# Two-layer graph attention: the last division of layer 1 in two parts, stepped along with the output projection, and the last output rows stored 128 at a time

## The chip, the cores and the metric

The kernel runs on one core of a Trainium2 chip. The metric is the device time of one execution in microseconds, as the median of several runs. All data are 32-bit floats.

## The reference

x is 4096 x 512, adj is 4096 x 4096. Both layers are residual attention layers over 4096 nodes with eight heads of 64. Cut to what matters here, which is the second layer (the first has the same outline, with additive scores):

```python
h = relu(layernorm(x))
keys, queries, values = h @ Wks, h @ Wqs, h @ Wvs        # per head: 4096 x 64
atts = queries @ keys.T / 8 - 1e16 * (1 - max(adj, I))   # per head: 4096 x 4096
atts = softmax(atts)
x = x + einsum('hqm,hmk,hko->qo', atts, values, Wo)      # sum over heads, 512 -> 512
```

## The kernel before

**Names.** TensorE (PE) does matmuls, VectorE (DVE), ScalarE (ACT) and GpSimd (POOL) the elementwise work, and every DMA of this part is issued by SyncE (SP), whose queue is worked in order: a DMA that waits for a semaphore holds all that stand behind it.

**Layer 1's main loop.** The eight heads are worked as `HC` = 4 pairs c. For each pair the 4096 queries are cut into `NG` = 32 groups of 128, and each group into `GS` = 4 sets of 32 queries, so there are `SETS` = 128 sets per pair and `total` = 512 sets. The order of the whole layer is written out by hand: one loop over steps s, in which a set goes through scores on PE (`scores`, L997), mask and minimum on DVE (`masked`, L1013), the exponential on ACT (`exps`, L1050, which also leaves the row sums in the tile `sums`), transposes on DVE and PE (`squares`, L1057; `turned`, L1065), and the product with the values (`weighted`, L1083) on PE. The product runs `PROD` = 8 steps behind, so n = s - 8 is the set that it works. After a group's four sets `finish` (L1092, L1093) copies the undivided result, transposed, to `att_d[c]` in DRAM. The penalties of a set (`a`, 512 KB, L963) are fetched 5 steps ahead.

**The division.** The softmax denominators are applied afterwards, for half a pair (16 groups, 2048 queries) at a time, by a generator `divided(c, half)` that does one small piece at each call of `next`. `inverted` sums the row sums across partitions with a matmul by `bands` into `tot` (L1098) and takes the reciprocal on DVE (L1103); at the next call it transposes the result on PE (L1106), copies it on ACT (L1108) and writes it to `inv_d` in DRAM with two DMAs (L1110). `scaled` then handles four blocks of 512 queries in two pairs of blocks: it loads the block of `att_d` (L1122, 256 KB) and the inverses, broadcast to 64 partitions, with two DMAs (L1124), each block at a call of its own; then multiplies both blocks (L1131); then stores both back to `att_d` (L1134). The multiplications are done by POOL, but by DVE in the very last division. A half costs eleven calls. A division starts at each n with n % 64 == 1 (n > 1), that is one step after its half is complete, and every step of the loop makes one call. Seven of the eight halves so lie inside the loop; the eighth, pair 3's second half, starts at s = 521, and the loop ends with s = 522, after two of its eleven calls.

**The projection.** `projected(j)` makes 128 output rows (tile j of `NB` = 32): eight PE instructions (four matmuls of 128 x 512, each recorded as two) into a PSUM tile `oo` (L1166; the pool has four buffers), then the residual is added on DVE (L1169). Two tiles make a chunk. A chunk's inputs, `at` (L1154, 512 KB of `att_d`, all pairs) and `xt` (L1156, 512 KB), are fetched by `load_chunk`, which is called three times at s = 508 to 510 and afterwards after each odd tile, which also stores the chunk's 256 rows (L1171, 512 KB). So chunk i + 3 is fetched when chunk i is done. Tiles 0 to 9 are made inside the loop (s = 513 to 522), tiles 10 to 31 in a plain loop after it. Chunks 0 to 7 cover groups 0 to 15, whose division is done early. Before `load_chunk` fetches chunk 8 or a later one, it first runs every division that is still open to its end, which for the eighth half means its nine open calls, all in a row:

```python
if i >= NG // 2 // ZR:
    for d in divisions:
        for _ in d:
            pass
    divisions.clear()
```

Chunk 8 is fetched after tile 11, in the plain loop. The functions that the diff touches, and their callers:

Of the kernel before, what the change touches and what calls it, by code (L numbers as in the profile page):

```python
# [15 lines left out]
P = 128  # L16
# [7 lines left out]
def kernel(  # L24
# [14 lines left out]
    nc = tc.nc  # L39
    N, DM = x.shape  # L40
    H, D = src_proj.shape[1:]
    HD = H * D
    NB = N // P
    KC = DM // P
    HC = HD // P
# [16 lines left out]
    SQ = 32  # L62
# [3 lines left out]
    bands = const.tile([P, P], F32, name="bands")  # L66
# [34 lines left out]
    with tc.tile_pool(name="a0k", bufs=1) as pk, tc.tile_pool(name="a0v", bufs=4) as pv, tc.tile_pool(  # L101
# [361 lines left out]
        def step(n):  # L463
            return groups[n // 2], n % 2

        with tc.manual_schedule():
            NQ = NB // XR
            rows = [load_rows(0)]
# [10 lines left out]
            made = []  # L479
# [10 lines left out]
            for q in range(NQ + 3):  # L490
                n = q - 3
# [8 lines left out]
                if n in (2, 4, 6):  # L500
                    for h in range(2):
                        cols = bass.ts(n // 2 - 1, 2 * XR * P)
# [29 lines left out]
            for s in range(total + 6):  # L532
                G, h = step(s) if s < total else (None, 0)
                for half in range(2):
# [3 lines left out]
                    n = 2 * s + half - LEAD  # L538
                    turn = 0 <= n < 2 * total
                    if turn:  # L540
                        T, i = groups[n // HALVES], n % HALVES
# [11 lines left out]
                    if half == 1 and s + 1 < total:  # L553
                        leaky(*step(s + 1))

                        c, at = divmod(s + 3, 2 * NB)
# [11 lines left out]
                    if 1 <= n <= 2 * total:  # L568
                        W, w = groups[(n - 1) // HALVES], (n - 1) % HALVES
# [13 lines left out]
    GS = P // SQ  # L583
    NG = NB
# [6 lines left out]
    with tc.tile_pool(name="b0c", bufs=1) as pc, tc.tile_pool(name="b0a", bufs=4) as pa, tc.tile_pool(  # L591
# [250 lines left out]
        with tc.manual_schedule():  # L842
# [4 lines left out]
            for s in range(SETS + PROD + 10):  # L847
                if s + AHEAD < SETS:
                    adjs[s + AHEAD] = load_adj(*step(s + AHEAD))
                n = s - PROD  # L850
# [20 lines left out]
                if s % 2 and s < SETS:  # L871
                    G, k = step(s)
# [3 lines left out]
                if s % 2 == 0 and 0 <= s - 2 < SETS:  # L876
                    G, k = step(s - 2)
# [3 lines left out]
                if 0 <= n < SETS:  # L881
                    W, w = step(n)
# [7 lines left out]
    inv_d = dram.tile([HC, 2, N], F32, name="inv_d")  # L890
# [15 lines left out]
    SG = NG // 2  # L906
    with tc.tile_pool(name="a1t", bufs=1) as pt, tc.tile_pool(name="a1k", bufs=4) as pkk, tc.tile_pool(
# [9 lines left out]
        sums = pt.tile([P, HC, 2, 2, SG, GS], F32, name="sums")  # L917
# [174 lines left out]
            nc.scalar.copy(oT, G.o[:, :P])  # L1092
            nc.sync.dma_start(att_d[G.c, :, bass.ts(G.g, P)], oT)  # L1093

        def inverted(c, half):

            tot = pm.tile([P, 512], F32, tag="ms", name="tot")
            nc.tensor.matmul(  # L1098
                tot[:, : 2 * SG * GS], lhsT=bands,
                rhs=sums[:, c, half].rearrange("p h g k -> p (h g k)"), start=True, stop=True,  # L1100
            )
            inv = px.tile([P, P], F32, tag="oT", name="inv")
            nc.vector.reciprocal(inv[:SQ], tot[:SQ, : 2 * SG * GS])  # L1103
            yield
            invT = pm.tile([P, 512], F32, tag="ms", name="invT")
            nc.tensor.transpose(invT[:, :SQ], inv[:SQ], ident[:SQ, :SQ])  # L1106
            rows = px.tile([P, SQ], F32, name="rows")
            nc.scalar.copy(rows, invT[:, :SQ])  # L1108
            for h in range(2):
                nc.sync.dma_start(  # L1110
                    inv_d[c, h, bass.ts(half, SG * P)].rearrange("(q i) -> q i", i=SQ), rows[bass.ts(h, D)]
                )
            yield

        def scaled(c, half):

            last = (c, half) == (HC - 1, 1)
            zs = []
            for i in range(4):
                cols = bass.ts(half * 4 + i, 4 * P)  # L1120
                z = pz.tile([P, 2, 4 * P], F32, tag="z", name="z")
                nc.sync.dma_start(z[:, 0], att_d[c, :, cols])  # L1122
                for h in range(2):
                    nc.sync.dma_start(z[bass.ts(h, D), 1], inv_d[c, h, cols].partition_broadcast(D))  # L1124
                yield
                zs.append((cols, z))
                if i % 2 == 0:
                    continue
                yield
                for cols, z in zs:  # L1130
                    (nc.vector if last else nc.gpsimd).tensor_mul(z[:, 0], z[:, 0], z[:, 1])  # L1131
                yield
                for cols, z in zs:
                    nc.sync.dma_start(att_d[c, :, cols], z[:, 0])  # L1134
                zs = []

        def divided(c, half):
            yield from inverted(c, half)
            yield from scaled(c, half)

        ZR = 2
        chunks = []

        def load_chunk():

            i = len(chunks)
            if i >= NG // 2 // ZR:
                for d in divisions:
                    for _ in d:
                        pass  # L1150
                divisions.clear()
            if i < NB // ZR:
                at = pat.tile([P, HC, ZR * P], F32, name="at")
                nc.sync.dma_start(at, att_d[:, :, bass.ts(i, ZR * P)].rearrange("c p n -> p c n"))  # L1154
                xt = pa.tile([P, ZR, DM], F32, tag="a", name="xt")
                nc.sync.dma_start(xt, x1_d[bass.ts(i, ZR * P), :].rearrange("(r p) d -> p r d", p=P))  # L1156
                chunks.append((at, xt))

        def projected(j):
            if j >= NB:  # L1160
                return
            i, r = divmod(j, ZR)
            at, xt = chunks[i]
            o = psc.tile([P, HF], F32, tag="sc", name="oo")
            for c in range(HC):
                nc.tensor.matmul(  # L1166
                    o, lhsT=at[:, c, bass.ts(r, P)], rhs=wot[:, c, :], start=(c == 0), stop=(c == HC - 1)
                )
            nc.vector.tensor_add(xt[:, r], xt[:, r], o)  # L1169
            if r == ZR - 1:  # L1170
                nc.sync.dma_start(out[bass.ts(i, ZR * P), :].rearrange("(r p) d -> p r d", p=P), xt)  # L1171
                load_chunk()

# [14 lines left out]
        with tc.manual_schedule():  # L1188
            pens = {}

            def prefetch(n):
                if n < total:
                    if n % (QG * GS) == 0:
                        load_queries(n // (QG * GS))
                    pens[n] = penalty(*step(n))

            AHEAD = 5
            rb = 0
            divisions = []
            load_keys(0)  # L1200
            for n in range(AHEAD):
                prefetch(n)
            for n in range(2):
                without_self(*step(n), pens[n])
                made_penalty(*step(n), pens[n])
            for i in range(GS):
                load_values(0, i)
            for s in range(total + PROD + 3):
                if s + 2 < total:
                    without_self(*step(s + 2), pens[s + 2])  # L1210
                if s < total:
                    keep_penalty(*step(s), pens[s])

                c, at = divmod(s + 4, SETS)
                if 0 < c < HC and at == 0:
                    load_keys(c)
                c, at = divmod(s - PROD - 1 + GS, SETS)
                if 0 < c < HC and at < GS:
                    load_values(c, at)
                turn = 0 <= s - TURN < total  # L1220
                if turn:
                    squares(*step(s - TURN))
                turn = turn and (s - TURN) % 2

                if s % 2 and 0 <= s - 3 < total:
                    G, k = step(s - 3)
                    smallest(G, k // 2)
                if turn:
                    tr = turned(*step(s - TURN))
                n = s - PROD  # L1230
                if 0 < n <= total and n % GS == 0:
                    finish(groups[n // GS - 1])
                if s > total:
                    projected(rb)
                    rb += 1
                if s < total:
                    scs = scores(*step(s))
                    masked(*step(s), scs, pens.pop(s))
                if turn:
                    taken(*step(s - TURN), tr)  # L1240
                if 0 <= s - EXPS < total:
                    exps(*step(s - EXPS))
                if s + 2 < total:
                    made_penalty(*step(s + 2), pens[s + 2])
                if s % 2 and s < total:
                    G, k = step(s)
                    parted(G, k // 2)
                if 0 <= n < total:
                    W, w = step(n)
                    weighted(W, w)  # L1250
                if n > 1 and n % (SG * GS) == 1:
                    divisions.append(divided(*divmod(n // (SG * GS) - 1, 2)))
                for d in divisions[:1]:
                    if next(d, d) is d:
                        divisions.pop(0)
                if s == (HC - 1) * SETS + SETS // 2:
                    wot = pkk.tile([P, HC, DM], F32, tag="k", name="wot")
                    nc.sync.dma_start(wot, wo.rearrange("h d o -> (h d) o").rearrange("(c p) o -> p c o", p=P))
                if s > total - AHEAD and len(chunks) < 3:
                    load_chunk()  # L1260
                prefetch(s + AHEAD)

            for j in range(rb, NB):
                projected(j)


# [26 lines left out]
```

## Time and profile before

| what | us |
|---|---|
| median of three runs | 4854.54 |
| fastest and slowest of them | 4853.94, 4856.94 |
| the profiled execution, its own time | 4850.36 |
| its span, from the first to the last instruction | 4848.6 |
| PE busy | 4663.8 (96%) |
| DVE busy | 4440.2 (92%) |
| ACT busy | 3833.9 (79%) |
| POOL busy | 440.3 (9%) |

The profiled execution lasted 1.8 us longer than its span, and 4.2 us less than the median of the runs. All start times below are microseconds from the span's start. Layer 1's loop fills the stretch from 2472 on; the tiles after the loop begin at 4757.8. In rows of the timeline the first two numbers are the start and the duration of a group of like instructions; what stands in brackets is the time for which the engine had been idle before it, and what ended that. In the table by stretches, the columns are the stretch, its length, then busy time and number of instructions for PE, PE's weight loads, DVE, ACT and POOL, and at last the granted clock of PE (1.00 is full), the share of the DMA engines, and the GB/s that they moved.

### The profile page before, as it was taken

The page shows a single profiled execution, that of the slowest core. Times are in us where ns is not written, and L with a number is a line of the kernel's source. Part 1 is how long each engine was busy: PE and PEld are TensorE (multiplying, and loading weights), DVE is VectorE, ACT ScalarE, POOL GpSimd, SP SyncE. Part 2 cuts the span into 40 slices and gives each one's busy share as a digit, 9 for nine tenths or more (in the row PEclk, how much of TensorE's full clock was granted, in tenths as well). Part 3 has the DMA queues.
Part 4 walks back from the last instruction along what each step waited for, and adds up shares of the span by engine and source line. Part 5 has one row for each costly group of instructions (what it writes and reads, how often), then busy time and mean ns, then how long its engine had stood idle before and what let it go on. Part 6 is the DMA issues. An engine that isn't in the chain of part 4 may idle for free.

```text
span 4848.6 us, 145764 instructions
## 1 busy us (share of the span) xinstructions
PE 4663.8 (96%) x62099; PEld 3480.4 (72%) x62099; DVE 4440.2 (92%) x7787; ACT 3833.9 (79%) x4300; POOL 440.3 (9%) x999
## 2 busy tenths in 40 slices
PE   8999999999999959999989999999999999999998
PEld 7888888888888847777756666666666666666664
DVE  7999999999999898988759999999999999999981
ACT  6999999999999898888648888666666666666660
POOL 2000000000000011100123343000000000000000
PEclk9999999999999979999999999999999999999999
DMA  7444544445444384444377787534344343544435
GB/s 267 151 165 152 183 169 161 158 150 202 162 157 150 119 183 141 148 140 146 107 224 253 251 277 262 183 130 152 136 161 158 132 158 129 192 132 139 154 123 196
DMA packets 358556, 818.49 MB, mean 169 GB/s; under 512 B 60048, under 2 KB 179088, under 8 KB 332816
## 3 DMA queue, kind: packets, MB, share of 16 engines
q1 hardware_dynamic: 357904, 809.16, 50.7%
q8 instruction: 486, 7.96, 0.7%
q14 instruction: 166, 1.36, 0.1%
HBM read 668.21 MB, written 140.77 MB: 167 GB/s over the span
## 4 chain that ended last, share of the span: by engine, by line
PE 61%; DVE 14%; ACT 13%; issue 8%; DMA 3%; SPq 1%; POOL 0%; DVEq 0%; ACTq 0%; POOLq 0%
PE o L1083 20%; PE sc L997 19%; ACT t L173 6%; PE tr L1065 5%; PE mp L793 5%; DVE t L163 5%; DVE pT L197 4%; ACT t L152 4%; ACT pT L195 2%; PE bo L716 2%; PE tr L186 2%; PE o L208 2%; DVE bt L669 2%; PE oo L1166 2%; DVE bt L708 2%
## 5 line engine op out<-in xcount | busy, mean ns | idle before, releaser
L1013 DVE CUSTOM_DVE_ANT_0 t<-sc,a 128x512 f32<-128x512 f32 x2048 | 1284.3, 682 | 88.9 <-PE sc L997 67.0
L1083 PEld LDWEIGHTS o<-t,v 128*64 128x64 f32 x16384 | 883.8, 137 | 428.4 <-issue 344.7
L1050 ACT ACTIVATE t<-t,nm 128x1024 f32<-128x1024 f32 x1024 | 1166.0, 1143 | 4.2 <-DVE nm L1039 3.6
L997 PE MATMUL sc<-k,q 64*32 64x512 f32 x16384 | 1004.5, 596 | 5.5 <-DVE nm L1013 5.4
L1083 PE MATMUL o<-t,v 128*64 128x128 f32 x16384 | 1007.4, 276 | 0.5 <-ACT oT L1092 0.4
L1057 DVE STREAM_TRANSPOSE t<-t 128x1536 f32<-128x1536 f32 x512 | 907.4, 1772 | 7.9 <-ACT t L1050 7.6
L163 DVE CUSTOM_DVE_ANT_0 t<-t,a 128x2048 f32<-128x2048 f32 x384 | 876.7, 2283 | 22.6 <-ACT t L152 18.3
L186 PE MATMUL tr<-ident,t 128*128 128x128 f32 x6144 | 779.2, 277 | 30.1 <-ACT pT L195 20.2
L208 PE MATMUL o<-pT,v 128*64 128x128 f32 x12288 | 757.1, 276 | 1.1 <-DVE pT L197 1.0
L186 PEld LDWEIGHTS tr<-ident,t 128*128 128x128 f32 x6144 | 662.6, 141 | 121.4 <-issue 65.5
L173 ACT ACTIVATE t<-t,nm 128x4096 f32<-128x4096 f32 x192 | 730.7, 3806 | 11.8 <-DVE nm L168 11.6
L152 ACT ACTIVATE t<-tb,src 128x4096 f32<-128x4096 f32 (+1 forms) x193 | 731.0, 3788 | 2.2 <-DVE tb L408 2.2
L1072 ACT COPY t<-tr 128x1024 f32<-128x1024 f32 x256 | 259.1, 1012 | 591.2 <-PE tr L1065 591.1
L208 PEld LDWEIGHTS o<-pT,v 128*64 128x64 f32 x12288 | 664.4, 137 | 62.0 <-issue 47.9
L197 DVE COPY pT<-tr 128x1024 f32<-128x1024 f32 x549 | 653.2, 1215 | 9.8 <-PE tr L186 9.8
L997 PEld LDWEIGHTS sc<-k,q 64*32 64x32 f32 x16384 | 251.6, 106 | 383.0 <-issue 331.0
L669 DVE CUSTOM_DVE_ANT_0 bt<-lk,ba 128x1024 f32<-128x1024 f32 x256 | 302.7, 1219 | 64.1 <-ACT e L799 45.3
L659 ACT ACTIVATE lk<-tb,srcb 128x1024 f32<-128x1024 f32 x256 | 283.7, 1116 | 74.5 <-DVE nm L669 65.7
L708 DVE STREAM_TRANSPOSE bt<-bt 128x2048 f32<-128x2048 f32 x128 | 295.0, 2306 | 0.0
L701 ACT ACTIVATE bt<-bt,nm 128x1024 f32<-128x1024 f32 x256 | 290.1, 1134 | 0.0
L1065 PE MATMUL tr<-ident,t 128*128 128x128 f32 x2048 | 280.4, 280 | 0.0
L716 PE MATMUL bo<-bt,bv 128*64 128x128 f32 x4096 | 257.8, 280 | 9.1 <-ACT boT L725 7.7
(123 smaller groups left out, 3656.1 us busy)
## 6 DMA issues: line engine op xcount, KB each, us to landing
a<-in_adj_dram SPq DMA_DIRECT2D x192, 1024.0 KB
a<-pen_d SPq DMA_DIRECT2D x384, 512.0 KB
ba<-in_adj_dram SPq DMA_DIRECT2D x512, 128.0 KB
a<-in_adj_dram SPq DMA_DIRECT2D x512, 128.0 KB
pen_d<-a SPq DMA_DIRECT2D x128, 512.0 KB
h<-hT_d SPq DMA_DIRECT2D x96, 256.0 KB
qk_d<-e SPq DMA_DIRECT2D x64, 256.0 KB
x<-in_x_dram SPq DMA_DIRECT2D x8, 1024.0 KB
```

What stands on the lines that cost most here:

```text
L152: nc.scalar.activation(tpart, targets[G.c, h][:, cols], AF.Prelu, bias=src[:, G.g, 2 * G.c + h : 2 * G.c + h + 1], alpha=SLOPE,)
L163: nc.vector.tensor_tensor_reduce(out=t, in0=t, in1=rows_of_adj[G, f], scale=-1.0, scalar=FMAX, op0=ALU.add, op1=ALU.min, accum_out=nm[:, f ...
L173: nc.scalar.activation(G.t[h], G.t[h], AF.Exp, bias=G.nm[h][:, NCH : NCH + 1], scale=-1.0, accum_out=G.sm[:, h : h + 1],)
L186: nc.tensor.transpose(tr[:, bass.ts(b % 4 * 2 + h, P)], G.t[h][:, bass.ts(i * MB + b, P)], ident)
L197: nc.vector.tensor_copy(pT, tr)
L208: nc.tensor.matmul(G.o[h * D : (h + 1) * D, :P], lhsT=feats[G.c][i][:, b, bass.ts(h, D)], rhs=pT[:, bass.ts(b % 4 * 2 + h, P)], start=(mb ...
L997: nc.tensor.matmul(sc[h][bass.ts(a, SQ), :], lhsT=G.q[bass.ts(h, D), bass.ds(G.q0 + k * SQ, SQ)], rhs=keys[G.c][half][bass.ts(h, D), a, :] ...
L1013: nc.vector.tensor_tensor_reduce(out=t[:, G.ring + k, h, cols], in0=scs[half][h], in1=a[:, cols], scale=1.0, scalar=FMAX, op0=ALU.add, op1 ...
L1050: nc.scalar.activation(u, u, AF.Exp, bias=G.nm[k // 2][:, k % 2, h : h + 1], scale=-1.0, accum_out=G.sm[:, h, k : k + 1],)
L1057: nc.vector.transpose(u, u)
L1065: nc.tensor.transpose(tr[:, j, h, bass.ts(m, P)], t[:, G.ring + k - 1 + j, h, bass.ds(VC + m * P, P)], ident,)
L1083: nc.tensor.matmul(G.o[bass.ts(h, D), :P], lhsT=v[:, b, bass.ts(h, D)], rhs=t[:, bass.ds(G.ring, GS), h, bass.ds(at, SQ)], start=(mb == 0) ...
```

## The change

A division now takes a first group g and a number of groups n instead of a half. The first seven half-pair divisions keep their place and size. Pair 3's second half becomes two divisions of eight groups. The first, of groups 16 to 23, starts at n = 481 (s = 489), inside the loop, and multiplies on POOL; the second, of groups 24 to 31, starts at s = 521, where the eighth half started before, and multiplies on DVE. Each has one pair of blocks, so seven calls instead of eleven. As the transpose works on 128 columns, the unused 64 columns of `inv` are set to one by a memset on DVE.

After the loop, `some_divided()` makes one call after each projected tile. `load_chunk` runs open divisions to their end from chunk 12 on instead of chunk 8. The last two tiles (j = 30 and 31) are each stored by a DMA of 128 rows (256 KB) instead of together.

```diff
-        def inverted(c, half):
+        def inverted(c, g, n):
+            half, w = g // SG, n * GS
...
-                tot[:, : 2 * SG * GS], lhsT=bands,
-                rhs=sums[:, c, half].rearrange("p h g k -> p (h g k)"), start=True, stop=True,
+                tot[:, : 2 * w], lhsT=bands, rhs=sums[:, c, half, :, bass.ds(g % SG, n), :],
+                start=True, stop=True,
...
-            nc.vector.reciprocal(inv[:SQ], tot[:SQ, : 2 * SG * GS])
+            if 2 * w < P:
+                nc.vector.memset(inv[:SQ, 2 * w :], 1.0)
+            nc.vector.reciprocal(inv[:SQ, : 2 * w], tot[:SQ, : 2 * w])
...
-        def scaled(c, half):
-            last = (c, half) == (HC - 1, 1)
+        def scaled(c, g, n):
+            last = c == HC - 1 and g + n == NG
...
-            for i in range(4):
-                cols = bass.ts(half * 4 + i, 4 * P)
+            for i in range(n // 4):
+                cols = bass.ds((g + 4 * i) * P, 4 * P)
...
+        def due(made):
+            c, g = divmod(made, NG)
+            if g == 0 and 0 < c < HC:
+                divisions.append(divided(c - 1, SG, SG))
+            elif g == 0 and c == HC:
+                divisions.append(divided(c - 1, NG - SG // 2, SG // 2))
+            elif g == SG:
+                divisions.append(divided(c, 0, SG))
+            elif (c, g) == (HC - 1, NG - SG // 2):
+                divisions.append(divided(c, SG, SG // 2))
+
+        def some_divided():
+            for d in divisions[:1]:
+                if next(d, d) is d:
+                    divisions.pop(0)
...
-            if i >= NG // 2 // ZR:
+            if i >= (NG - SG // 2) // ZR:
...
-            if r == ZR - 1:
+            if j >= NB - ZR:
+                nc.sync.dma_start(out[bass.ts(j, P), :], xt[:, r])
+            elif r == ZR - 1:
...
-                if n > 1 and n % (SG * GS) == 1:
-                    divisions.append(divided(*divmod(n // (SG * GS) - 1, 2)))
-                for d in divisions[:1]:
-                    if next(d, d) is d:
-                        divisions.pop(0)
+                if n > 1 and n % GS == 1:
+                    due(n // GS)
+                some_divided()
...
             for j in range(rb, NB):
                 projected(j)
+                some_divided()
```

More of the change, by code (lines that the diff above doesn't have):

```diff
@@ L1110, in inverted @@
                 nc.sync.dma_start(
-                    inv_d[c, h, bass.ts(half, SG * P)].rearrange("(q i) -> q i", i=SQ), rows[bass.ts(h, D)]
+                    inv_d[c, h, bass.ds(g * P, n * P)].rearrange("(q i) -> q i", i=SQ), rows[bass.ts(h, w)]
                 )
             yield
-        def scaled(c, half):
-            last = (c, half) == (HC - 1, 1)
+        def scaled(c, g, n):
+            last = c == HC - 1 and g + n == NG
             zs = []
-            for i in range(4):
-                cols = bass.ts(half * 4 + i, 4 * P)
+            for i in range(n // 4):
+                cols = bass.ds((g + 4 * i) * P, 4 * P)
                 z = pz.tile([P, 2, 4 * P], F32, tag="z", name="z")
@@ L1135, in scaled, with divided @@
                 zs = []
-        def divided(c, half):
-            yield from inverted(c, half)
-            yield from scaled(c, half)
+        def divided(c, g, n):
+            yield from inverted(c, g, n)
+            yield from scaled(c, g, n)
+        divisions = []
+        def due(made):
[12 more added lines that the diff above has]
+                    divisions.pop(0)
         ZR = 2
@@ L1198 @@
             rb = 0
-            divisions = []
             load_keys(0)
```

## The prediction

> **What bounds the kernel now.** I read the page first, for which engine fills the span and whose work the chain that ended last is made of.
>
> ```profile
> span 4848.6 us, 145764 instructions
> ...
> PE 4663.8 (96%) x62099; PEld 3480.4 (72%) x62099; DVE 4440.2 (92%) x7787; ACT 3833.9 (79%) x4300; POOL 440.3 (9%) x999
> ...
> PE 61%; DVE 14%; ACT 13%; issue 8%; DMA 3%; SPq 1%; POOL 0%; DVEq 0%; ACTq 0%; POOLq 0%
> ```
>
> PE sets the pace nearly everywhere, and only 3% of the chain is DMA. So I looked for where the chain leaves PE in the part that the change touches: first the table by stretches after the loop, then the chain of waits there.
>
> ```profile
> 4757.00:4778.00 21.00, 21.00 (x50) 9.17 (x49) 3.45 (x5) 0.18 (x1) 0.00 (x0) 1.00 0.63 207
> 4778.00:4787.00 9.00, 0.87 (x3) 0.20 (x2) 3.78 (x6) 0.00 (x0) 0.00 (x0) 0.83 0.68 196
> 4787.00:4792.00 5.00, 5.00 (x8) 2.20 (x9) 0.00 (x0) 0.00 (x0) 0.00 (x0) 0.63 1.04 392
> ```
>
> In the second row PE works 0.87 of 9 us; in the third it is busy again, but its granted clock is 0.63.
>
> ```profile
> 4763.69 1.30 PE oo L1166 x3
> ...
> 4767.61 3.94 DMA z<-inv_d
> ...
> 4772.36 2.00 DMA att_d<-z
> ...
> 4777.05 3.61 DMA z<-inv_d
> ...
> 4781.97 4.72 DMA at<-att_d
> ...
> 4786.83 1.19 PE oo L1166
> ```
>
> From tile 11 on the chain is the eighth half's division, run to its end in one go: loads of two blocks, multiply, store, again, and only then (4781.97) the fetch of chunk 8, for which PE waits until 4786.83. PE had chunks 5 to 7 to work on meanwhile, which lasted to 4778.7. The idle time is 8.1 us.
>
> **Step 1, the stall: -10.3 us.** I take its price from the additions of the residual, one for each tile, in DVE's timeline.
>
> ```profile
> 4765.01 0.69 DVE L1169 TENSOR_TENSOR xt<-xt,oo 128x512 f32<-128x512 f32 x1 [2.74 <-PE oo L1166]
> ...
> 4792.47 0.69 DVE L1169 TENSOR_TENSOR xt<-xt,oo 128x512 f32<-128x512 f32 x1 [8.51 <-PE oo L1166]
> 4795.90 0.69 DVE L1169 TENSOR_TENSOR xt<-xt,oo 128x512 f32<-128x512 f32 x1 [2.75 <-PE oo L1166]
> ```
>
> They are those of tiles 11, 16 and 17. A tile that waits for nothing takes 4795.90 - 4792.47 = 3.43 us. Five tiles should take 17.2 us; tiles 12 to 16 took 27.46. The loss is 10.3: 8.1 idle, and some 2.2 in which PE ran at the lower clock.
>
> With the change nothing runs the division in one go. Its seven calls fall on s = 521, 522 and tiles 10 to 14: loads after tiles 10 and 11, multiplications after 13, stores after 14. Chunk 12, the first that needs these groups, is fetched after tile 19, five tiles (17 us) later. Chunk 8 is fetched right after tile 11, about 4766.5, and needed at tile 16, 4778.7. What the step puts into each queue after the loop: on SP three issues after tile 10 (0.46 + 0.81 + 0.56 = 1.8 us, like those at 4766.16 to 4768.17), three more behind chunk 8's fetch after tile 11, two stores after tile 14. The first broadcast load must wait for the inverses to land in DRAM. They were issued from 4760.97 to 4762.08 behind a 1 MB chunk fetch; as nothing waited for them in this trace, I bound the landing by rows: 2 us after issue (the store at 4772.36) to 4.7 (the fetch at 4781.97), so 4764 to 4767. This holds SP by at most a microsecond or two past the store of chunk 5 at 4765.73 and delays chunk 8's fetch by as much, against 12 us of room less 4.7 us of transfer. Cover left: 5 us or more. On DVE the two multiplications (0.69 each) stand after tile 13's addition, near 4772, and wait for blocks issued by 4770 that land 3.6 to 3.9 us later: DVE may wait 1 to 2 us, with 2.75 us idle after each tile anyway, and PE has four PSUM tiles to go on with. I take zero. What is late next is PE's own pace of 3.43 us a tile.
>
> **Step 2, the last store: -0.8 us.** After the last addition SP issues the store of 512 KB at 4844.68, and its wait at the end of the program (2.2 us, from 4845.22) ends at 4847.45.
>
> ```profile
> SPq L1289 <- DMA out_dram<-xt: 2.2, 1, 2.2
> ```
>
> From issue to landing that is 2.77 us. A store of 256 KB, also from 128 partitions, is in the chain above: 2.00 us (4772.36). Tile 30's half goes 3.43 us earlier, beside PE's last tile. So 0.77 is saved; the bounds are 0 and 0.8.
>
> The Trainium skill's page DMA: Bandwidth & Descriptors, section Anatomy of one DMA, fits a DMA of the GpSimd path as 2.0 us plus its bytes at 436 GB/s, and its section Bandwidth advises transfers of 1 MiB and more, which speaks against cutting this one. By that fit, as an estimate, halving would save 0.6 us, and the whole sum would come out 0.2 us smaller; the rows here are for SP's own DMAs, so I go by them.
>
> **Step 3, one more division inside the loop: +1.1 us.** Seven such divisions are in the trace at the same place of the four-step cycle; pair 3's first starts in step s = 457. DVE's first mask of steps 455, 457, 461 and 463:
>
> ```profile
> 4457.91 0.69 DVE L1013 CUSTOM_DVE_ANT_0 t<-sc,a 128x512 f32<-128x512 f32 x1 [0.25 <-PE sc L997]
> 4466.57 0.69 DVE L1013 CUSTOM_DVE_ANT_0 t<-sc,a 128x512 f32<-128x512 f32 x1 [0.25 <-PE sc L997]
> ...
> 4469.69 0.94 DVE L1103 RECIPROCAL inv<-tot 32x128 f32<-32x128 f32 x1 [0.59 <-PE tot L1098]
> ...
> 4485.07 0.69 DVE L1013 CUSTOM_DVE_ANT_0 t<-sc,a 128x512 f32<-128x512 f32 x1 [0.19 <-PE sc L997]
> 4493.73 0.69 DVE L1013 CUSTOM_DVE_ANT_0 t<-sc,a 128x512 f32<-128x512 f32 x1 [0.25 <-PE sc L997]
> ```
>
> Two steps take 8.66 us before and after. Four steps across the division take 18.50 instead of 17.32: it costs 1.18. PE's timeline says where: the two matmuls of `tot` put 0.42 ahead of the next scores (4469.17 to 4469.59), and the transpose with ScalarE's copy, on which the next `nmB` waits, puts in 0.7. The later calls cost nothing: the steps after it are back at 8.66 while the loads, POOL's multiplications (1.29 each) and the stores run. The new division is half as wide. Two matmuls of `tot` start 0.11 apart for 128 columns, and those of 512 columns 0.43 apart, so 64 columns save 0.05 each, 0.1 together: +1.07. If DVE set the cost, its halved reciprocal would save 0.47 of 0.94: +0.7 is the lower bound, +1.18 the upper. The memset has no row here; the small reduction of `nm` (0.15) and this reciprocal (0.94) bound it, and it hides in DVE's wait of 0.59 for `tot`; uncovered it would add 0.15 to 0.35. Moved past in the loop: on SP ten issues (two inverses, six loads, two stores), behind which penalties queue that are wanted five steps, 21.7 us, later; POOL's two multiplications take 2.6 us of an engine that has 0.24 us of work in 8.66. The existing halves issue eighteen and four, without a lengthened step.
>
> **Step 4.** The division after the loop has the half-width `tot`: -0.1. The second half of its loads and stores has gone into the loop and off the path with step 1.
>
> **The sum.** -10.3 - 0.8 + 1.1 - 0.1 = -10.1 us on the profiled execution: span 4848.6 to 4838.5, own time 4850.36 to 4840.3. That execution is 4.2 us under the median of the runs, which I take as an offset that stays: 4854.5 - 10.1 = 4844.4, or -0.21%. I count 0.2% (9.7 us) as what can be told from no change, and the forecast sits just beyond that.
>
> **The rivals.**
>
> (A) The forecast, 4844.4, chance 0.76. Its own range is 4842.5 to 4847: the bounds of steps 2 and 3, and the spread of the runs (-0.6 to +2.4).
>
> (B) A shorter stall stays, chance 0.13. The division's transfers now run beside chunk 8's fetch, through the same SP queue. For: the third stretch shows the DMA engines full (share 1.04, 392 GB/s) when fetches bunch, and one took 4.72 us. Against: the room of 12 us. If SP is held for some 10 us at the first broadcast load, PE stands for about 3 us, and with the low clock after it (2.2) half of step 1 is lost: near 4849.5. The Trainium skill's page TensorE: Matmul & The Clock Gate, section Part 1, says that the clock falls after an idle window of about 3.4 us, counted freely. By that rule a stall of 3 us may pass at full clock, and (B) would give about 4847.4; no stall of that length is in the rows above.
>
> (C) The change does not do what it says, chance 0.05: a division is still open at chunk 12 and is run out there. Then its one pair of blocks (4766.16 to 4774.4 for such a pair before, 8.2 us) lies under three chunks of fetched work (20.6 us less 4.7 of fetch), so even then little comes back: 4845 to 4846.
>
> (D) Slower, chance 0.06: DVE's multiplications stand ahead of tile 14's addition, and their wait for the broadcast inverses takes the place of the stall. PE runs out of PSUM tiles at tile 18 (near 4785), so the wait costs nothing until the blocks land later than 4784, and is worse than before from a landing of about 4794, some 25 us after issue. The rows show 3.6 to 3.9. A landing 30 us after issue would give 4859.
>
> **Chances and range.** A's centre is only 0.4 us past the 0.2%, so a little over 6 in 10 of A and half of C count as faster: 0.50. The rest of A, B and C are within: 0.44. D is slower: 0.06. The range runs from A's low end, 4842, to B's 4849.5, and leaves D and A's edges out.
>
> **What would show it.** Right: additions at even 3.43 us from tile 10 to 31; granted clock 1.00 to the end; no wait of PE for `at`; four steps across s = 489 at 18.4 us; the wait at the end of the program near 1.5 us. Wrong: PE idle before tile 16 or any later one; SP held at the first load of inverses beyond 4770; a step lengthened in s = 491 to 500; or runs whose offset to the profiled execution differs, since the margin to 0.2% is smaller than their spread.

## The result, and the profile after

| | before | after |
|---|---|---|
| median of nine runs, us | 4854.54 | 4841.45 |
| fastest and slowest | 4852.03, 4856.94 | 4839.5, 4844.75 |
| profiled execution, span | 4848.6 | 4837.7 |

The ratio is 0.9973, with a 95% interval of 0.9963 to 0.9983: faster by 13 us, of which the interval leaves 8 to 18. The forecast of 4844.4 had the direction, but the time lies 0.55 us below the range (4842 to 4849.5). The spans differ by 10.9.

The page of the changed kernel, the same three lines:

```profile
span 4837.7 us, 145786 instructions
...
PE 4660.0 (96%) x62102; PEld 3477.0 (72%) x62102; DVE 4439.3 (92%) x7788; ACT 3834.3 (79%) x4301; POOL 442.8 (9%) x1001
...
PE 60%; DVE 16%; ACT 14%; issue 8%; DMA 2%; SPq 1%; POOL 0%; DVEq 0%; ACTq 0%; POOLq 0%
```

On the page little is to be seen: the chain holds 1% less DMA. The table by stretches of the changed kernel shows where it went:

```profile
4757.00:4778.00 21.00, 21.00 (x50) 9.17 (x49) 4.04 (x6) 0.19 (x1) 0.00 (x0) 1.00 0.78 249
4778.00:4787.00 9.00, 9.00 (x22) 3.99 (x21) 3.26 (x5) 0.00 (x0) 0.00 (x0) 1.00 0.85 297
4787.00:4792.00 5.00, 5.00 (x13) 2.28 (x12) 0.69 (x1) 0.00 (x0) 0.00 (x0) 1.00 0.94 312
```

PE is busy through the second and third stretch, at full clock. The DMA engines move more than before in the second (297 GB/s against 196) and less in the third (312 against 392), so the transfers have spread under the matmuls. PE's timeline has the 22 tiles after the loop in one unbroken row:

```profile
4757.75 75.80 PE L1188 MATMUL oo<-wot,at 128*128 128x512 f32 x176
```

DVE's timeline of the changed kernel, from tile 11 on (L1191 is the addition, L1134 the division's multiplication):

```profile
4764.92 0.69 DVE L1191 TENSOR_TENSOR xt<-xt,oo 128x512 f32<-128x512 f32 x1 [2.75 <-PE oo L1188]
...
4772.40 0.69 DVE L1134 TENSOR_TENSOR z<-z 128x512 f32<-128x512 f32 x1
4778.61 0.69 DVE L1134 TENSOR_TENSOR z<-z 128x512 f32<-128x512 f32 x1 [5.53 <-DMA z<-inv_d]
4779.22 1.28 DVE L1191 TENSOR_TENSOR xt<-xt,oo 128x512 f32<-128x512 f32 x2
4782.09 0.69 DVE L1191 TENSOR_TENSOR xt<-xt,oo 128x512 f32<-128x512 f32 x1 [1.59 <-PE oo L1188]
```

Tile 16's addition starts 17.17 us after tile 11's, five times 3.43; before, it took 27.46. The additions of tiles 14 and 15 were late (4779.22, both in one row), as the second multiplication waited 5.53 us for its inverses, but PE did not wait for them.

In the loop, the part that starts in step s = 489 (first masks of s = 487, 489, 491 and 493):

```profile
4596.44 0.69 DVE L1013 CUSTOM_DVE_ANT_0 t<-sc,a 128x512 f32<-128x512 f32 x1 [0.25 <-PE sc L997]
4605.10 0.69 DVE L1013 CUSTOM_DVE_ANT_0 t<-sc,a 128x512 f32<-128x512 f32 x1 [0.25 <-PE sc L997]
4607.58 0.11 DVE L1105 MEMSET inv<- 32x64 f32 x1
4608.17 0.55 DVE L1106 RECIPROCAL inv<-tot 32x64 f32<-32x64 f32 x1 [0.47 <-PE tot L1099]
4614.89 0.69 DVE L1013 CUSTOM_DVE_ANT_0 t<-sc,a 128x512 f32<-128x512 f32 x1 [0.35 <-PE sc L997]
4623.55 0.69 DVE L1013 CUSTOM_DVE_ANT_0 t<-sc,a 128x512 f32<-128x512 f32 x1 [0.25 <-PE sc L997]
```

Two steps that take 8.66 took 9.79: 1.13 us. And the waits of SP from tile 10 to the end (name, what it waited for, us, times, longest):

```profile
SPq L1127 <- DMA inv_d<-rows: 3.9, 1, 3.9
...
SPq L1312 <- DMA out_dram<-xt: 2.0, 1, 2.0
```

SP was held for 3.9 us at the first load of inverses, and the wait at the end of the program was 2.0 instead of 2.2. That wait also starts some 0.2 us sooner after the last store's issue, so from issue to landing the last store took 2.3 us instead of 2.75.

To compare stages, I cut each trace at the first mask of s = 487, two steps ahead of the first thing that the change moves:

| stage, us | before | after | difference |
|---|---|---|---|
| start to pair 0's first mask | 2472.14 | 2470.04 | -2.10 |
| pair 0 | 563.88 | 564.77 | +0.89 |
| pair 1 to s = 487 | 1561.64 | 1561.63 | -0.01 |
| s = 487 to s = 511 | 103.92 | 105.05 | +1.13 |
| to the last addition's end | 143.08 | 132.79 | -10.29 |
| to the span's end | 3.93 | 3.44 | -0.49 |

From s = 487 on the change is worth 9.65 us. Another 1.2 us of the spans' difference lies in stages that the change does not touch, and the timed medians are 2 us further apart still. So **theory 1**: the change works as worked out, and what is beyond it is chance of single executions in untouched stages. **Theory 2**: the change also moves untouched stages, for instance by where its code or data come to lie.

### The profile page after: what moved, and what is told of

It is laid out like the page before. It is cut to its first block, busy times and chain, and to the rows that moved or that the text cites. A ratio compares the mean times of both kernels' runs of the same rounds, so it can differ in the third digit from the quotient of the medians.

```text
span 4837.7 us, 145786 instructions
## 1 busy us (share of the span) xinstructions
PE 4660.0 (96%) x62102; PEld 3477.0 (72%) x62102; DVE 4439.3 (92%) x7788; ACT 3834.3 (79%) x4301; POOL 442.8 (9%) x1001
## 4 chain that ended last, share of the span: by engine, by line
PE 60%; DVE 16%; ACT 14%; issue 8%; DMA 2%; SPq 1%; POOL 0%; DVEq 0%; ACTq 0%; POOLq 0%
PE o L1083 20%; PE sc L997 19%; ACT t L173 6%; DVE t L163 6%; PE tr L1065 5%; PE mp L793 5%; DVE pT L197 4%; ACT t L152 4%; ACT pT L195 2%; PE bo L716 2%; PE oo L1188 2%; DVE bt L669 2%; PE tr L186 2%; PE o L208 2%; DVE bt L708 2%
```

## The experiments

### The kernel before, again

No edit.

> The kernel before, unchanged, as a measure of what differs with nothing changed. Theory 1 (the change is worth 9.65 us, all of it from step s = 487 on; the other 3.4 us between the medians are chance of the runs in stages that the change does not touch): the stretch from the first mask of s = 487 to the end is 250.9 us again within 0.1, and what lies ahead of it (4597.7 us in the first profile) differs by 1 to 3 us. Theory 2 (the change also moves untouched stages, by where its code or data lie): both stretches repeat within 0.5 us, and the medians of the kernel before repeat at 4854 to 4855.

Measured: from s = 487 on 251.11 us, ahead of it 4601.68, that is 4.0 more than in the first profile with nothing changed. The median of 11 runs was 4853.31; 30 runs of the same kernel beside it gave 4852.71. This is theory 1's picture, though neither stretch kept to its limits: the last one was 0.2 us longer instead of 0.1 at most (see below), and the one ahead of it differed by more than 3.

### The changed kernel, again

No edit.

> The changed kernel, unchanged, again. Theory 1: from the first mask of s = 487 to the end 241.3 us within 0.1 again; the ratio moves from 0.9973 towards 0.9980 (9.65 of 4854). Theory 2: the stretch ahead of s = 487 is 1.2 us or more below that of the kernel before once more, and the ratio stays at 0.9973, about 13 us.

Measured: from s = 487 on 241.29; ahead of it 4599.93, 3.5 above the first profile's. The ratio is 0.9977 (0.9966 to 0.9987), the medians 4841.65 and 4852.71, 11.1 us apart. The ratio lies between the two expectations, and ahead of s = 487 the changed kernel is once more below the kernel before, by 1.75 us, as theory 2 had it. This is not enough to decide.

### The single stores alone

```diff
-            if r == ZR - 1:
+            if j >= NB - ZR:
+                nc.sync.dma_start(out[bass.ts(j, P), :], xt[:, r])
+            elif r == ZR - 1:
```

> Of the change only the last two tiles' stores of 128 rows; the division as before. From the last addition's end to the span's end: 3.44 us as in the changed kernel instead of 3.93, so -0.5 us (the prediction said -0.8). The stall before tile 16 as before: tile 11's addition to tile 16's 27.5 us. In the timed runs no difference that can be told (theory 1); theory 2 would allow some 3 us by another layout.

Measured: the end after the last addition 3.49 us instead of 3.92 (-0.4). The last store landed 2.0 us after its issue instead of 2.75, so 0.7 came off there; but from its landing to the span's end it took 1.45 instead of 1.15. Timed 4854.0 beside 4852.71, ratio 1.0000 (0.9992 to 1.0009): nothing that can be told. From s = 487 on it took 251.89, 1 us more than the first profile of before, though the end is shorter: the stall, which this edit leaves in place, cost 11.7 us here instead of 10.3.

### The division alone

The changed kernel, with that edit taken back.

> The change without the single stores of the last two tiles. From s = 487 to the end: 250.9 + 1.13 - 10.29 = 241.8 us, and the end after the last addition 3.93 us as before. Timed: -9.2 us, ratio 0.9981 by theory 1; 0.9974 by theory 2.

Measured: s = 487 to 511 105.05, then 132.79 to the last addition, as in the changed kernel to the hundredth, and an end of 4.18, where 3.93 was expected: 242.02 in all. The ratio is 0.9982 (0.9973 to 0.9991). The division makes nearly all of the gain.

### Run to the end later, without calls after the loop

```diff
                 projected(j)
-                some_divided()
```

> The changed kernel without the calls after the loop's tiles: the second part of the division is run out in one go when chunk 12 is fetched, after tile 19. Theory 1 (the split alone nearly hides it, since one pair of blocks takes 8.2 us and the fetch 4.9, against the 13.7 us that chunks 10 and 11 last): PE idle before tile 24 for 0 to 2 us, s = 487 to the end 241.3 to 243.5 us. Rival (the stepping is what removes the stall): some 8 us idle and the low clock after it, near 251 us.

Measured: 243.14 us from s = 487 on, 1.8 more than the changed kernel. PE's waits after the loop, and the stretches around the one it has, in this kernel:

```profile
PE oo L1188 <- DMA at<-att_d: 1.5, 1, 1.5
```

```profile
4803.00:4812.00 9.00, 7.46 (x19) 3.07 (x18) 1.38 (x2) 0.00 (x0) 0.00 (x0) 1.00 0.98 324
4812.00:4834.00 22.00, 22.00 (x53) 9.66 (x51) 4.13 (x6) 0.00 (x0) 0.00 (x0) 1.00 0.53 188
```

So the split, with the run to the end moved to chunk 12, brings 8 of the 10 us by itself in this one profile; the calls after each tile bring the last 1.8. And a pause of 1.5 us left the clock at 1.00, where in the stretch after one of 8.1 the granted clock had been 0.63.

### Stepped, not split

```diff
             for j in range(rb, NB):
                 projected(j)
+                for d in divisions[:1]:
+                    if next(d, d) is d:
+                        divisions.pop(0)
```

on the kernel before.

> The kernel before with a call of the open division after each tile, and nothing split: the run to its end still comes when chunk 8 is fetched, and only the first block's loads go ahead of it. Theory 1: the loads wait for the inverses to land near 4765.7, so 0 to 2 us of the 8.1 are saved, s = 487 to the end 249 to 251 us. Rival (stepping alone does it): near 242 us.

Measured: 251.38 us from s = 487 on, no better than before, and just above the 249 to 251 expected. PE's wait:

```profile
PE oo L1166 <- DMA at<-att_d: 9.0, 1, 9.0
```

Stepping does nothing while chunk 8 still has to wait for four blocks.

### The first part begun after the loop's last masks

```diff
-            elif (c, g) == (HC - 1, NG - SG // 2):
+            elif (c, g) == (HC - 1, NG - 2):
```

in the changed kernel.

> The changed kernel with the first part of the last division begun at s = 513 instead of 489, so that its seven calls stand beside tiles 0 to 6. Theory 1 (the part costs 1.13 us in the loop because the next scores and the next minimum wait behind it on PE, and only PE's own 0.3 us beside the tiles): s = 487 to 511 103.9 us instead of 105.05, to the last addition 133.1 instead of 132.8, s = 487 to the end 240.5 us, no idle PE before tile 16. Rival (it now stands too near chunk 8's fetch, and its loads and stores delay it): a stall of some us before tile 16, 243 us or more. In the timed runs 0.8 us less than the changed kernel, which they can't tell.

Measured: s = 487 to 511 103.92, then 133.19 and 3.51: 240.62 in all, 0.66 less than the changed kernel, with no wait of PE for `at`. The loop's 1.13 went, and 0.4 came back beside the tiles. Timed 4842.24 beside 4855.65, ratio 0.9974 (0.9964 to 0.9983), against 0.9973 of the changed kernel: the runs cannot tell the two apart, the trace can.

### Ten more sums and transposes in the loop

```diff
+                if n // GS >= (HC - 1) * NG and n // GS - (HC - 1) * NG in range(1, 11) and n % GS in (1, 2):
+                    if n % GS == 1:
+                        more = inverted(HC - 2, 0, SG // 2)
+                    next(more)
                 some_divided()
```

> The changed kernel with ten more of the first two calls of a division of eight groups (sums, reciprocal, transpose, two stores of the inverses, which write the same values again), one in each of ten groups of pair 3. Theory 1: each costs 1.1 us, set by PE, so the stretch from pair 1's start to s = 487 grows from 1561.6 by 11 us (10 to 12). Rival (VectorE sets it, and half a reciprocal costs half): 7 us.

Measured: 1572.90 instead of 1561.63 us, 11.27 for ten: 1.13 each. First masks of steps 397, 399 and 401, with the first of them, and below PE's part of it:

```profile
4211.25 0.69 DVE L1013 CUSTOM_DVE_ANT_0 t<-sc,a 128x512 f32<-128x512 f32 x1 [0.20 <-PE sc L997]
4214.32 0.55 DVE L1106 RECIPROCAL inv<-tot 32x64 f32<-32x64 f32 x1 [0.47 <-PE tot L1099]
4221.04 0.69 DVE L1013 CUSTOM_DVE_ANT_0 t<-sc,a 128x512 f32<-128x512 f32 x1 [0.35 <-PE sc L997]
4229.70 0.69 DVE L1013 CUSTOM_DVE_ANT_0 t<-sc,a 128x512 f32<-128x512 f32 x1 [0.25 <-PE sc L997]
```

```profile
4213.84 0.43 PE L1099 MATMUL tot<-sums,bands 128*128 128x64 f32 x2
4214.21 1.95 PE L997 MATMUL sc<-k,q 64*32 64x512 f32 x32
...
4217.98 0.24 PE L1109 MATMUL invT<-ident,inv 32*128 32x32 f32 x1
4218.59 0.31 PE L1034 MATMUL nmB<-parts,bands 128*64 128x32 f32 x4 [0.37 <-ACT rows L1111]
```

Two steps take 9.79 us with one of them and 8.66 without, and the halved reciprocal (0.55 for 0.94) took nothing off beyond 0.05. So DVE does not set the price. It is put into PE's order, as the sum had it: the sums (L1099) put 0.37 us ahead of the next scores, and the transpose (L1109) with PE's wait of 0.37 for ScalarE's copy puts 0.61 ahead of the next `nmB`.

### Two more pairs of both kernels

No edits; four runs beside each other.

> The kernel before once more, for the stretch ahead of s = 487, beside the changed kernel on the same chip. Theory 1: ahead of s = 487 somewhere in 4595 to 4602 us, from there to the end 250.9 to 252.3 us (what the stall costs varies with when the full clock comes back). Theory 2 (code or data of the change move untouched stages): 1.5 us or more above the changed kernel's in both pairs.

> The changed kernel once more. Theory 1: from s = 487 to the end 241.3 us a third time, ahead of it somewhere in 4595 to 4602 us, with no order between the two kernels; the timed difference 10 to 11 us, ratio 0.9978 to 0.9980. Theory 2: ahead of s = 487 below the kernel before in both pairs, the timed difference 13 us, ratio 0.9973.

> The kernel before, the second of two pairs. Theory 1: ahead of s = 487 in 4595 to 4602 us, then 250.9 to 252.3 us to the end. Theory 2: 1.5 us or more above the changed kernel's ahead of s = 487.

> The changed kernel, the second of two pairs. Theory 1: 241.3 us from s = 487 to the end, and ahead of it no order against the kernel before. Theory 2: below the kernel before ahead of s = 487 by 1.5 us or more.

Measured, with the first two profiles of each kernel (ahead of s = 487, and from there on):

| | before | after |
|---|---|---|
| first | 4597.65, 250.92 | 4596.44, 241.28 |
| again | 4601.68, 251.11 | 4599.93, 241.29 |
| third | 4598.61, 252.28 | 4604.78, 241.29 |
| fourth | 4601.24, 251.26 | 4600.06, 241.24 |
| mean | 4599.8, 251.39 | 4600.3, 241.27 |

Ahead of s = 487 there is no order between the kernels: in three pairs the changed kernel is 1.2 to 1.75 us below, in the third it is 6.2 above, at 4604.78, outside the 4595 to 4602 that was expected. The means differ by 0.5 us the other way from theory 2. So nothing here speaks for theory 2; but with a scatter of 4 us in one kernel and 8 in the other, eight profiles can't exclude a shift of 1 to 3 us. What the change moves is worth 251.39 - 241.27 = 10.1 us. The timed ratios of these two pairs were 0.9976 (0.9968 to 0.9985) and 0.9978 (0.9970 to 0.9987), and over all four pairs the medians are 11 to 13 us apart; 10.1 would be 0.9979, inside each of the four intervals of the changed kernel.

## Why the prediction was wrong, and where it was right

**The step that failed is the one from the profile to the runs:** "4.2 us under the median of the runs, which I take as an offset that stays". It did not stay. The profiled execution of the changed kernel took 4839.5 us, 1.95 under its median of 4841.45, and this difference of 2.2 is most of the 3 us by which the forecast was too high. The rest is in the profiled execution itself, 0.8 us below its forecast of 4840.3: the touched stages gave 9.65 instead of 10.1, but 1.2 more went in stages that the change does not touch. In the six later profiles of the two kernels the profiled execution lies 0 to 7.2 us above the median of its runs, so there is no offset that could be carried over. A differing offset was among the prediction's own signs of being wrong, but its range left only 2.4 us below the forecast, while single executions of the same code differ by up to 8 us ahead of s = 487 (4596.44 to 4604.78 for the changed kernel). What makes them differ is not shown.

The base was less at fault. 4854.54 was a median of three runs, and nine runs beside the changed kernel gave it again; elsewhere medians of the same kernel were 4852.7 (30 runs), 4853.3 (33) and 4855.65 (13). The four medians of the changed kernel lie between 4840.6 and 4842.5. The chances were made with the same narrow margin: six in ten for "beyond 0.2%" came from a centre 0.4 us past it. Between the timed differences (11 to 13) and the traces' 10.1, 1 to 3 us stay open.

The sum's -10.1 is also the mean over four profiles of each kernel, but that is partly luck: the stall was worth some 0.5 us more than forecast, the last store 0.3 less, and step 4 nothing.

**Step 1, the stall (-10.3).** It was right as a mechanism, and to the hundredth for the pair of first profiles (10.29). But its size is not fixed: against 132.79 in the changed kernel, the four profiles of before lose 10.29, 10.48, 11.65 and 10.63, mean 10.8; the one I had was the cheapest. PE was idle for 8.1, 8.8, 8.8 and 8.6 us of it, and the remaining 2.2, 1.7, 2.9 and 2.0 go with the lower clock. In the third profile of before:

```profile
4783.00:4793.00 10.00, 4.58 (x6) 2.03 (x7) 2.78 (x5) 0.00 (x0) 0.00 (x0) 0.53 0.82 267
4793.00:4800.00 7.00, 7.00 (x17) 3.05 (x16) 1.38 (x2) 0.00 (x0) 0.00 (x0) 0.95 0.73 266
```

Well inside the stretch of the lower clock (4784 to 4793 here, 4784 to 4790 in the first profile) the granted clock is 0.50. If it is either full or half, 0.53 over 10 us and 0.95 over 7 are 9.4 and 0.7 us of half clock, 10.1 together; the first profile's 0.83 over 9 and 0.63 over 5 are 3.1 and 3.7, or 6.8. The Trainium skill's page TensorE: Matmul & The Clock Gate, section Part 1, has just that: an idle state at half the clock and a busy one at full, and windows of about 3.4 us that run freely; 6.8 and 10.1 are two and three of them, so the trace agrees. The prediction's 2.2 is what the half clock cost, not how long it lasted.

**Step 2, the last store (-0.8).** Mis-sized: -0.49 in the first pair, -0.4 alone. The price of 2.00 us for the store was near: it landed 2.0 us after issue in the run of the stores alone and 2.3 in the changed kernel, against 2.75 before. But the time from landing to the span's end, which the sum left as it was, differs between the kernels (1.15 before, 1.1 in the changed kernel, 1.45 with the stores alone), and the wait at the end was 2.0, not near 1.5. The Trainium skill's page DMA: Bandwidth & Descriptors, section Anatomy of one DMA, gave 0.6 as an estimate by the slope of its fit for the GpSimd path, nearer to the 0.4 to 0.5 than my 0.8.

**Step 3, the part in the loop (+1.07).** It cost 1.13, and ten more gave 1.13 each. The halved width saved 0.05 instead of 0.11. The memset (0.11) hid as said.

**Step 4 (-0.1).** It brought nothing: from the first mask of s = 511 to tile 11's addition, across these sums, both kernels take 63.44 us.

**The room after the loop.** Chunk 8's fetch met no stall. SP was held until 4765.74, inside the 4764 to 4767 forecast. The wait of DVE for the last inverses was 5.53 us, not 1 to 2: the last load was issued at 4770.19 and landed 8.4 us later, not 3.6 to 3.9, beside the fetches of chunks 8 and 9. So half of (D)'s mechanism came, and cost nothing, since the four PSUM tiles were there as forecast. With it the sign "additions at even 3.43 us" failed for tiles 14 and 15.

**The rivals.** (B) did not come. Its price took in the clock's loss; the one short pause on record, of 1.5 us, left the clock at 1.00, and no run has a pause of 3. (C) was nearly tried by the late run to the end: 1.8 us over the changed kernel, against 0.6 to 1.6 forecast. The working had three chunks of cover; it is two (10 and 11, 13.7 us), and 1.5 us of wait came through. The same slip is in step 1's "chunks 5 to 7": between tile 11 and 4778.7 PE had the four tiles of chunks 6 and 7.

## What to carry to other kernels

A generator that is run to its end in front of a fetch puts its whole chain of DMA round trips on that fetch; look for the first consumer that really needs its result, and split the work so that only the part that this consumer needs is in front of it. Split first, then step: the stepping alone gave nothing, the split alone eight tenths, in one profile each. For a gain of some 0.2%, cut the traces into stages and compare the touched ones over several profiles: stages where PE sets the pace repeat to 0.01 us, while the untouched start and pair 0, where DMA shares near 1 are seen, wander by several microseconds (that the one makes the other is not shown); take the base from many runs, and a range no narrower than single executions.

## What the runs showed of the hardware beyond that

The cost of one and the same pause of PE varied by 1.4 us with nothing changed, in part through the idle time (8.1 to 8.8 us) and in part through the time at half clock (6.8 us in the first profile, 10.1 in the third). Loads of 128 KB that landed 3.6 to 3.9 us after issue in one place took 8.4 us where the DMA engines moved 250 to 300 GB/s. The last store landed 2.75 us after issue with 512 KB in every profile, and 2.0 to 2.3 with 256 KB; from its landing to the span's end it took another 0.84 to 1.45. Profiles of one kernel agree in that to about 0.01 us, while kernels that end with the same two stores do not (1.1 in the changed kernel, 1.45 in the stores alone). Why is not shown.
